# Summing the first two row tiles of an edge table during the load, ahead of the sums in DRAM

## The chip, the cores and the metric

The kernel runs on one core of one Trainium2 chip. The metric is the device time of one execution in microseconds, from the first to the last instruction on the core and what lies around them. The engines have short names in the profile: PE is TensorE (matrix products; PEld is its loading of weights), DVE is VectorE, ACT is ScalarE, POOL is GpSimd, SP is SyncE. DMA transfers are issued by SP, ACT or POOL.

## The reference

One layer of a graph transformer on 1,250 nodes with 768 features, all in float32. Three branches follow each other, cut here to what is computed:

```python
xn = layernorm(x)
x = x + gnn(xn, src, dst) + mix(xn)      # mix: linear attention, then an MLP with gelu
x = x + ffn(layernorm(x))                # 2 of 4 experts, chosen by the mean of all nodes

def gnn(x, src, dst):                    # 21,250 edges, loops of the nodes added to them
    x1 = gat(layer_norm(x), W1, heads=4, width=192)
    x2 = gat(x1, W2, heads=2, width=96)
    return concat(x, x2) @ Wu + bu

def gat(x, W, ...):
    h = x @ W
    e = leaky_relu(s_src[src] + s_dst[dst])
    ee = exp(e - segment_max(e, dst)[dst])
    return segment_sum(ee / segment_sum(ee, dst)[dst] * h[src], dst) + bias
```

What concerns the change is the attention over edges: for each destination node a maximum over its incoming edges, and then a weighted sum. An edge can occur more than once, and counts as often as it occurs.

## The kernel before, in words

**The edges' table.** The kernel turns the list of edges into a dense table of 1,250 by 1,250 counts (row: source node, column: destination node). It is built in DRAM by 170 indirect DMAs of POOL with addition (L315), 125 edges each. They go by turns into two tables, `tabs[0]` and `tabs[1]`, so that a scatter need not wait for the one just ahead of it. `halves[0]` and `halves[1]` are the two tables as 1,250 rows of 1,250 values; `adj_d` is another name for `halves[0]`.

**The two tables become one.** `merged(c)` (L1112) adds the rows of tile c, 125 rows, of the second table to those of the first, with one accumulating DMA from DRAM to DRAM (L1115). Ten such sums make the whole table, 610 KB each.

**The first pass over the table.** `largest` (L1119) finds each destination's maximum, over the ten row tiles. For every tile POOL fetches 610 KB to the chip (`fetch`, L1128), by turns into three buffers: two at the back of `slot_x` and one in `turns`. VectorE makes `far` of it (L1143, no edge becomes a large negative number), and then for each of four heads a running maximum (L1151 for the first tile, L1147 for the others). At the start `before`, here `merged`, is called for tiles 0, 1 and 2, and then `fetch` for tiles 0 and 1. In the loop, step c sums tile c + 3, fetches tile c + 2 and works on tile c. `largest` runs a second time for the second attention layer, with two heads and no sums; it then reads the finished table, as `weighted` does for both layers (L1203).

**What sets the order.** POOL, like each engine, works its instructions in order, and a DMA that has to wait for another one's landing waits on POOL itself. The DMAs of `merged` and `fetch` are held in program order (`pin`). The scatters stand ahead of them on POOL. The work of `gnn` is laid between the steps of the mixing MLP by a credit: `gnn()` is a generator that yields what its last step costs in microseconds, `spend` (L1366) adds to a credit as TensorE's work is written, and takes the next step of `gnn` when the credit is enough. It starts at -44. `largest` yields 9.0 after the first DMAs and 5.0 for every two heads. So VectorE's instructions of `largest` stand at fixed places between those that empty TensorE's banks for the MLP: `fc2_half` (L1077 the products, L1082 the addition of their sum to `slot_a`), and `fc1_unit` (L1046, L1059, L1066).

**The buffers.** `slot_x[:TP, 5000:7500]` holds the first two tiles of three; the running maxima of four heads are in `slot_x[:TP, :5000]`. The queries that lay in `slot_x` before are last read by the projection (L974), which ends before 521 us in the profile.

Of the kernel before, what the change touches and what calls it, by code (L numbers as in the profile page):

```python
# [12 lines left out]
ALU = mybir.AluOpType  # L13
AX = mybir.AxisListType

N, D, TP, NT, KC = 1250, 768, 125, 10, 6
# [16 lines left out]
def tile_gps_layer(ctx, tc, a, out):  # L33
    nc = tc.nc
# [20 lines left out]
    halves = [tab[0:PAIRS, :].rearrange("(s d) o -> s (d o)", d=N) for tab in tabs]  # L55
# [9 lines left out]
    slot_x = big.tile([128, NT * D], F32, name="slot_x")  # L65
# [6 lines left out]
    pin = tc.keep_in_program_order  # L72
# [12 lines left out]
    def bank(name):  # L85
        return p_mm[0].tile([128, 512], F32, name=name, tag="mm")
# [547 lines left out]
    with tc.tile_pool(name="kvp", bufs=1) as kvp:  # L634
# [187 lines left out]
        for t in range(5):  # L822
            def before(t=t):
                if t == 1:
                    by_tokens(vec, xt, TP, TP)
                if t == 2:
                    by_tokens(vec, xt, 2 * TP, 3 * TP)
                    for vv in vvs:
                        pin(nc.vector.memset(vv[:, :, 128:129], 1.0))
# [65 lines left out]
    with tc.tile_pool(name="qp", bufs=1) as qp:  # L895
# [70 lines left out]
        for part in order2:  # L966
# [27 lines left out]
            for t in part:  # L994
                z = qp.tile([TP, D], F32, name="z2", bufs=2)
                i = where[t]
# [111 lines left out]
    def rest(n):  # L1108
        for _ in range(n):
            yield 2.5  # L1110

    def merged(c):  # L1112
        if c < NT:
            cs = slice(c * TP, (c + 1) * TP)
            pin(nc.gpsimd.dma_start(  # L1115
                adj_d[cs, :], halves[1][cs, :], accum_op=ALU.add, max_dma_last_dim=N
            ))

    def largest(heads, s, b_d, pace, before=lambda c: None, behind=lambda: None):  # L1119


        run = slot_x[:TP, : heads * N].rearrange("p (h n) -> p h n", n=N)
        load = [slot_x[:TP, 5000 + i * N : 5000 + (i + 1) * N] for i in range(2)]
        load.append(turns[:TP, 0, :N])

        def fetch(c):
            if c < NT:
                pin(nc.gpsimd.dma_start(load[c % 3], adj_d[c * TP : (c + 1) * TP, :]))  # L1128

        for c in range(3):  # L1130
            before(c)
        fetch(0)
        fetch(1)
        yield 9.0
        for c in range(NT):
            before(c + 3)
            fetch(c + 2)
            if c == NT - 1:
                behind()
            adj = load[c % 3]  # L1140

            far = turns[:TP, 1, :N]
            pin(nc.vector.tensor_scalar(far, adj, -2.0 * NEG, NEG, op0=ALU.mult, op1=ALU.add))  # L1143
            for h in range(heads):
                sc = s[:, 0, h, c : c + 1]
                if c:
                    pin(nc.vector.scalar_tensor_tensor(  # L1147
                        run[:, h, :], far, sc, run[:, h, :], op0=ALU.min, op1=ALU.max
                    ))
                else:  # L1150
                    pin(nc.vector.tensor_scalar(run[:, h, :], far, sc, None, op0=ALU.min))  # L1151
                if h % 2:
                    yield pace
        yield from rest(2)
        mx = gp.tile([TP, heads, NT], F32, name=f"mx{heads}")
        for h in range(heads):
            for u0 in range(0, NT, 4):
                n = min(4, NT - u0)
                ps = bank("ps_mx").rearrange("p (u c) -> p u c", c=128)
                for u in range(n):  # L1160
                    pin(nc.tensor.transpose(
                        ps[:TP, u, :TP], run[:, h, (u0 + u) * TP : (u0 + u + 1) * TP],
                        ident[:TP, :TP],
                    ))
                nc.vector.tensor_reduce(
                    mx[:, h, u0 : u0 + n], ps[:TP, :n, :TP], AX.X, ALU.max
                )
            yield 2.0
        sd = s[:, 1]
        b = gp.tile([TP, 2, heads, NT], F32, name=f"b{heads}")  # L1170
        m = small.tile([TP, heads, NT], F32, name=f"m{heads}", bufs=1)
        nc.vector.tensor_tensor(mx, mx, sd, ALU.add)
        nc.vector.scalar_tensor_tensor(m, mx, 0.2, mx, op0=ALU.mult, op1=ALU.max)
        nc.vector.tensor_tensor(b[:, 0], sd, m, ALU.subtract)
        nc.vector.scalar_tensor_tensor(
            b[:, 1], sd, 0.2, m, op0=ALU.mult, op1=ALU.subtract
        )
        yield from rest(2)
        n = 2 * heads * NT
        ps = bank("ps_row")  # L1180
        pin(nc.tensor.transpose(
            ps[:n, :TP], b.rearrange("p j h t -> p (j h t)"), ident[:TP, :TP]
        ))
        row = small.tile([80, TP], F32, name="row", bufs=1)
        nc.vector.tensor_copy(row[:n], ps[:n, :TP])
        nc.scalar.dma_start(b_d, row[:n])
        yield from rest(4)
# [50 lines left out]
    def gnn():  # L1238
        feats = {}

        def fetch(h):
            gh = turns[:TP, h % 2, :].rearrange("p (t f) -> p t f", f=193)
            pin(nc.gpsimd.dma_start(gh, rows(g1_d[h % 4], TP)))
            feats[h % 4] = gh

        yield from largest(4, s1, b1_d, 5.0, merged, lambda: fetch(0))
        fetch(1)
        for g, (t0, n) in enumerate(SPLITS):
            for h in range(4):
# [15 lines left out]
                for i in range(n):  # L1265
# [9 lines left out]
                    if h == 3:  # L1275
                        for j in range(2):
# [5 lines left out]
                            nc.vector.tensor_reduce(s2[:, j, :, t0 + i], pr, AX.X, ALU.add)  # L1282
        nc.vector.tensor_scalar(s2l, s2[:, 0], 0.2, None, op0=ALU.mult)
        yield from largest(2, s2, b2_d, 4.5)
        load_wu2x()
        parts = earlier()
# [471 lines left out]
    for i in range(6):  # L1758
        for u in range(4):
            q, c = 2 * i + u // 2, u % 2  # L1760
# [100 lines left out]
```

## Time and profile before

| | |
|---|---|
| median of 3 runs | 1902.39 us (1890.05 to 1907.74) |
| the profiled execution | 1900.13 us |
| its span | 1898.2 us |
| TensorE busy | 1869.0 us (98%) |
| VectorE busy | 1336.0 us (70%) |
| POOL busy | 498.0 us (26%), 351.1 of it the 170 scatters of L315 |
| granted TensorE clock | 0.994 of full speed |
| sums in DRAM, L1115 | 10 of 610.4 KB, 12.9 us median to landing |
| fetches of the first pass and the second, L1128 | 20 of 610.4 KB, 6.6 us median to landing |

The page of the profile lists the busy time of each engine, the chain of work that ended last (each step followed back to what released it), the costliest groups of instructions, and the DMA issues. A row of the timeline or the chain begins with the start in microseconds from the span's start, and the duration; in the timeline the engine and the line of the kernel follow, what is written and read, how many such instructions, and in brackets how long the engine stood idle ahead of it and what ended that. A row of the waits reads: who waited, for whom, microseconds in total, times, longest. The releaser named in a wait is inferred; where the engine named had long been done, it was another, often a DMA. The execution profiled has 1.9 us around its span.

### The profile page before, as it was taken

Reading aid. Unit: us, or ns where it says so; the run is one execution under the profiler, and the core shown is the slowest. Engines: PE = TensorE matmul, PEld = TensorE weight load, DVE = VectorE, ACT = ScalarE, POOL = GpSimd, SP = SyncE. Lnnn points to the kernel's source line nnn. Section 1 sums busy time; section 2 is a strip of 40 time slices with the busy share of each in tenths; the row PEclk is TensorE's granted clock in tenths of the full one; section 3 lists DMA queues with packets and bytes.
Section 4 is the critical chain, followed back from the end, with each engine's and each line's share of the span. In section 5 each row is a group of like instructions: output and inputs, shape, how many; then the busy total and the mean of one; then the engine's idle time right before and its main releaser. Section 6 shows DMA issues by size and latency. Waiting matters only on the chain.

```text
span 1898.2 us, 19544 instructions
## 1 busy us (share of the span) xinstructions
PE 1869.0 (98%) x6966; PEld 1245.7 (66%) x6966; DVE 1336.0 (70%) x2407; ACT 803.3 (42%) x1207; POOL 498.0 (26%) x341
## 2 busy tenths in 40 slices
PE   9999999999998999999999999999999999999998
PEld 7555556865565668787777655566766666666664
DVE  4656692677546967676666977766677777777778
ACT  3233221331321128777674186645364353433330
POOL 2265766687882110111111121000221000000000
PEclk9999999999998999999999999999999999999999
DMA  9748532523139751233343532202485201011023
GB/s 341 238 97 213 114 85 52 134 19 49 2 30 187 136 145 55 70 95 88 106 113 79 151 111 73 69 9 67 126 101 82 71 0 67 3 64 47 12 87 109
DMA packets 184285, 175.50 MB, mean 92 GB/s; under 512 B 110043, under 2 KB 153595, under 8 KB 182908
## 3 DMA queue, kind: packets, MB, share of 16 engines
q0 software_dynamic: 126640, 68.01, 20.8%
q1 hardware_dynamic: 54270, 98.48, 16.4%
q10 hardware_dynamic: 3278, 7.75, 1.3%
q8 instruction: 55, 0.90, 0.2%
q14 instruction: 42, 0.34, 0.1%
HBM read 137.80 MB, written 42.05 MB: 95 GB/s over the span
## 4 chain that ended last, share of the span: by engine, by line
PE 91%; DMA 4%; POOL 1%; DVE 1%; issue 1%; ACT 1%; SPq 0%; DVEq 0%; POOLq 0%; ACTq 0%
PE ps_f L1077 14%; PE ps_p L81 13%; PE ps_r L81 12%; PE ps_o L1255 7%; PE ps_a L127 7%; PE ps_g L578 4%; PE ps_u L545 4%; PE ps_p L974 4%; PE ps_c L127 3%; PE ps_f L1655 3%; PE ps_o L1294 2%; PE ps_va L127 2%; PE ps_ka L127 2%; PE ps_qa L127 2%; PE ps_d L127 2%; POOL tab L315 1%
## 5 line engine op out<-in xcount | busy, mean ns | idle before, releaser
L315 POOL DMA_INDIRECT tab<-mult,place_e x170 | 351.1, 2065 | 157.7 <-DMA tab<-mult,place_e 102.6
L1077 PE MATMUL ps_f<-w,v 128*125 128x384 f32 x960 | 338.9, 487 | 6.9 <-DVE slot_a L1082 6.9
L1077 PEld LDWEIGHTS ps_f<-w,v 128*125 128x125 f32 x960 | 178.0, 188 | 113.4 <-DVE slot_a L1082 8.0
L1082 DVE TENSOR_TENSOR slot_a<-ps_f,slot_a 125x384 f32<-125x384 f32 x240 | 131.6, 553 | 66.6 <-PE ps_f L1077 62.7
L1210 DVE TENSOR_TENSOR wt<-ee 125x375 f32<-125x375 f32 (+1 forms) x180 | 105.9, 590 | 84.5 <-PE ps_o L1255 57.5
L1255 PEld LDWEIGHTS ps_o<-turns,wt 125*125 125x125 f32 x800 | 137.1, 188 | 29.1 <-DVE wt L1211 4.0
L1255 PE MATMUL ps_o<-turns,wt 125*125 125x193 f32 x800 | 151.7, 329 | 2.9 <-DVE wt L1211 2.9
L1205 ACT ACTIVATE ee<-bt,s 125x375 f32<-125x375 f32 (+1 forms) x180 | 114.8, 638 | 77.1 <-DVE wt L1210 69.8
L81 PE MATMUL ps_p<-fT,w 128*128 128x312 f32 (+1 forms) x432 | 125.5, 426 | 0.6 <-ACT c L1573 0.6
L1211 DVE SCALAR_TENSOR_TENSOR wt<-wt,slot_x 125x375 f32<-125x375 f32 (+1 forms) x180 | 105.9, 590 | 4.4
L81 PEld LDWEIGHTS ps_p<-fT,w 128*128 128x128 f32 x432 | 81.5, 189 | 36.2 <-ACT c L1573 1.1
L81 PE MATMUL ps_r<-w,slot_a 128*125 128x384 f32 x260 | 94.5, 486 | 0.0
L127 PE MATMUL ps_a<-fT,w 128*128 128x250 f32 (+1 forms) x288 | 86.8, 432 | 0.7 <-DVE slot_a L979 0.7
L1617 DVE SCALAR_TENSOR_TENSOR slot_x<-ps_r,gate,slot_x 125x384 f32<-125x384 f32 x100 | 60.7, 615 | 33.3 <-PE ps_r L81 33.0
L81 PE MATMUL ps_p<-xt,ws 128*128 128x313 f32 (+1 forms) x288 | 83.6, 426 | 0.0
L578 PE MATMUL ps_g<-fx,zT 128*125 128x388 f32 x240 | 80.2, 490 | 1.5 <-DVE zT L372 1.5
L545 PE MATMUL ps_u<-wu,fT 128*125 128x384 f32 x240 | 79.9, 487 | 0.4 <-ACT fT L531 0.4
L974 PE MATMUL ps_p<-wp,slot_x 128*125 128x384 f32 x240 | 79.9, 486 | 0.0
L1147 DVE SCALAR_TENSOR_TENSOR slot_x<-turns,s,slot_x 125x1250 f32<-125x1250 f32 x54 | 79.4, 1512 | 0.1
L1026 ACT ACTIVATE v<-v,par 128x250 f32<-128x250 f32 (+1 forms) x72 | 40.0, 556 | 88.0 <-DVE v L1046 41.3
L1208 ACT ACTIVATE ee<-bt,s1l 125x375 f32<-125x375 f32 (+1 forms) x120 | 75.4, 628 | 0.1
L81 PE MATMUL ps_r<-w2s,ht 128*125 128x384 f32 x200 | 72.7, 486 | 0.0
(403 smaller groups left out, 3413.0 us busy)
## 6 DMA issues: line engine op xcount, KB each, us to landing
turns<-g_d POOLq DMA_DIRECT2D x12, 942.4 KB, 14.2
w<-in_L_mix_fc_w_dram SPq DMA_DIRECT2D x12, 768.0 KB
w<-in_L_mix_fc_w_dram SPq DMA_DIRECT2D x24, 384.0 KB
slot_x<-tab POOLq DMA_DIRECT2D x14, 610.4 KB, 6.6
w<-in_L_ffn_w_dram SPq DMA_DIRECT2D x11, 768.0 KB
w<-in_L_ffn_w_dram SPq DMA_DIRECT2D x5, 1536.0 KB
slot_x<-tab POOLq DMA_DIRECT2D x40, 183.1 KB, 3.3
kr_l<-key_d SPq DMA_DIRECT2D x6, 1062.5 KB
```

What stands on the lines that cost most here:

```text
L81: return lambda *args, **kw: pin(getattr(self.engine, name)(*args, **kw))
L127: engine.matmul(ps, wt[:, k, :], x[:, k, :], start=k == 0 and not more, stop=k == n - 1, skip_group_check=more,)
L315: nc.gpsimd.indirect_dma_start(out=tabs[c % 2][:, :], out_offset=bass.IndirectOffsetOnAxis(ap=place[:, c : c + 1], axis=0), in_=mult[:, c ...
L545: nc.tensor.matmul(ps[:TP, :w], fT[:, k, tc_], wu[:, k, c0 : c0 + w], start=k == 0, stop=k == KC - 1,)
L578: nc.tensor.matmul(ps[:TP, :388], zT[:, k, :], fx[:, k, h2 * 388 : (h2 + 1) * 388], start=k == 0, stop=k == KC - 1,)
L974: nc.tensor.matmul(ps[:TP, :w], qT[:, k, t * TP : (t + 1) * TP], pm[:, k, c0 : c0 + w], start=k == 0, stop=k == KC - 1,)
L1077: nc.tensor.matmul(ps, v_of[c][:, f, h, at : at + TP], lasts[g, j][:, f, :], start=f == 0, stop=f == 1,)
L1082: nc.vector.tensor_tensor(o, ps, o, ALU.add)
L1205: nc.scalar.activation(e[:, 0, :w], bt[:TP, 0, :w], AF.Exp, bias=s[:, 0, h, c : c + 1])
L1210: nc.vector.tensor_tensor(wt[:, :w], e[:, 0, :w], e[:, 1, :w], ALU.max)
L1211: nc.vector.scalar_tensor_tensor(wt[:, :w], wt[:, :w], 1.0, adj, op0=ALU.min, op1=ALU.mult)
L1255: nc.tensor.matmul(sums[i // 2][:TP, (i % 2) * 193 : (i % 2 + 1) * 193], wt[:, i * TP : (i + 1) * TP], gh[:, c, :], start=c == 0 and i % 2 ...
```

## The change

For the first attention layer the first two row tiles do not come from the summed table any more. `merged(0)` and `merged(1)` each load the tile's rows of the first table into the buffer that the fetch filled before, and then load the same rows of the second table on top with an accumulating DMA. `merged(2)` then makes the sums in DRAM of tiles 0, 1 and 2, one after the other, by `merge` (the former `merged`). From tile 3 on `merged(c)` is `merge(c)` as before. `largest` calls `fetch` for tiles 0 and 1 only in its second run, with two heads. All ten sums in DRAM are still made, and all DMAs stay on POOL's queue in program order.

```diff
+    early = [slot_x[:TP, 5000 + i * N : 5000 + (i + 1) * N] for i in range(2)]
+
     def merged(c):
+        if c < 2:
+            rs = slice(c * TP, (c + 1) * TP)
+            pin(nc.gpsimd.dma_start(early[c], halves[0][rs, :]))
+            pin(nc.gpsimd.dma_start(
+                early[c], halves[1][rs, :], accum_op=ALU.add, max_dma_last_dim=N
+            ))
+        for c in ((), (), (0, 1, 2))[c] if c < 3 else (c,):
+            merge(c)
+
+    def merge(c):
         if c < NT:
             cs = slice(c * TP, (c + 1) * TP)
             pin(nc.gpsimd.dma_start(
...
         for c in range(3):
             before(c)
-        fetch(0)
-        fetch(1)
+        if heads == 2:
+            fetch(0)
+            fetch(1)
         yield 9.0
         for c in range(NT):
             before(c + 3)
```

## The prediction

> **What bounds the kernel now.** I read the page first, then the waits, then the chain of waits around the change, then the timeline there. The page's busy table says what a saving must be:
>
> ```profile
> span 1898.2 us, 19544 instructions
> PE 1869.0 (98%) x6966; PEld 1245.7 (66%) x6966; DVE 1336.0 (70%) x2407; ACT 803.3 (42%) x1207; POOL 498.0 (26%) x341
> ```
>
> TensorE is busy 98% of the span, so an edit to transfers is worth what it takes from TensorE's few gaps or adds to them. The waits between 540 and 720 us, where the edges' table is summed and first used, hold the largest gap of the whole run:
>
> ```profile
> DVE turns L1143 <- DMA slot_x<-tab: 10.5, 1, 10.5
> PE ps_f L1077 <- DVE slot_a L1082: 6.9, 1, 6.9
> ```
>
> VectorE stands 10.5 us in front of L1143, the first use of the summed table, until a DMA lands. Behind it in VectorE's order stand the L1082 additions that empty TensorE's banks, so TensorE stops for 6.9 us. The chain of waits shows what the DMA hangs on:
>
> ```profile
> 560.30 3.61 DMA tab<-mult,place_e
> 565.37 17.10 DMA tab<-tab
> 583.19 9.14 DMA slot_x<-tab
> ...
> 595.83 2.92 PE ps_f L1077 x4
> 598.75 3.32 PE ps_a L127 x6
> ```
>
> The last scatter lands at 563.9; the sums of the table in DRAM (tab<-tab, L1115) take to 582.5; the fetch takes to 592.3; TensorE runs again at 595.83. The last two rows also show its clock coming back: four matmuls took 2.92 where eight take 2.58 (1.63 lost), six took 3.32 where six take 1.89 elsewhere (1.43 lost). So this place costs 6.86 + 3.06 = 9.9 us, and no more can be won here. The timeline gives the order of the transfers (POOL issues them in program order) and the use of the first and the third tile:
>
> ```profile
> 564.44 4.63 POOL L1115 DMA_DIRECT2D tab<-tab  x3 [2.14 <-DMA tab<-mult,place_e]
> 576.00 0.57 POOL L1128 DMA_DIRECT2D slot_x<-tab  x1 [6.93 <-PE ps_f L1077]
> 583.19 0.54 POOL L1128 DMA_DIRECT2D slot_x<-tab  x1 [6.63 <-DMA tab<-tab]
> 583.72 1.54 POOL L1115 DMA_DIRECT2D tab<-tab  x1
> 589.42 0.55 POOL L1128 DMA_DIRECT2D turns<-tab  x1 [4.17 <-PE ps_f L1077]
> 590.54 0.96 DVE L1143 TENSOR_SCALAR turns<-slot_x 125x1250 f32<-125x1250 f32 x1 [10.53 <-DMA slot_x<-tab]
> 607.05 0.80 DVE L1143 TENSOR_SCALAR turns<-turns 125x1250 f32<-125x1250 f32 x1
> ```
>
> Three DRAM sums enter the queue at once. By their landings (and the fetches that wait for them) they end at 575.3, 582.5 and 588.8: 10.8 us for the first, then 7.2 and 6.35. The fetch of tile 0 goes out at 576.0 but lies behind sums 1 and 2 and lands only at 590.5. The fetch of tile 2 (the turns row) goes out when sum 2 has landed, with sum 3 ahead of it, and lands at 598.1, 9 us before VectorE wants it at 607.05.
>
> **The change, part by part.** Removed: the fetches of tiles 0 and 1 in the first pass. Added ahead of the three DRAM sums, on POOL: for each of these tiles a plain load of the first table's rows and an accumulating load of the second's. The accumulating load must wait until the plain one has landed, and all that POOL holds behind it waits too: the next pair, and the three DRAM sums, which are all still made because later passes read the summed table. Kept: tile 2 is fetched from DRAM after sum 2, behind sum 3.
>
> *Plain load.* Nearest rows, a fetch of the same 610 KB: 5.0 us on an empty queue (the shortest landing), 6.6 median.
>
> ```profile
> slot_x<-tab POOLq DMA_DIRECT2D x14, 610.4 KB, 6.6
> slot_x<-hx POOLq DMA_DIRECT2D x10, 375.0 KB, 23.0
> tab<-tab POOLq DMA_DIRECT2D x10, 610.4 KB, 12.9
> ```
>
> It needs the first table's scatters alone; the last of those was issued at 558.0 and lands some 3.7 us later, so POOL is free for it at about 562.8. It lands at 562.8 + 5.0 = 567.8.
>
> *Accumulating load.* Not in the trace. From below: a plain load, 5.0. From above: slot_x<-hx, an accumulation into the same memory; its first one took 19.2 us for 375 KB, though with four more behind it and with its source on chip. Nearest: the first DRAM sum, same bytes, same source table, same wait and nothing ahead of it, 10.8 us:
>
> ```profile
> DMA to landing us min/median/max: 10.8/10.8/10.8
> ```
>
> I take 10.84. Below nothing it cannot be: it is one more transfer.
>
> [...]
>
> *The sum.* POOL needs about 0.55 us from a landing to the next issue (575.3 to 576.0 in the trace).
> - Tile 0 is summed at 568.4 + 10.84 = 579.3. VectorE, which stopped at 580.02 before, has it in time: this wait is gone.
> - The load of tile 1 lies behind it in the queue and lands some 1.7 us later (as the fetch of tile 0 landed 1.7 after sum 2): 581.0. Its sum is in at 581.6 + 10.84 = 592.4. VectorE would want it at 596.16 - 9.9 = 586: 6 us late, within the 8.9 us that TensorE ran on after VectorE stopped (580.02 to 588.96). Cost nothing, with that cover; it would be at most 6 us without.
> - The three DRAM sums follow in the same queue at the pace of sums 1 and 2, (7.2 + 6.35) / 2 = 6.8 each: 592.4 + 20.3 = 612.7. Issuing them costs POOL 1.5 us each, beside the transfer of tile 1.
> - Tile 2 lands 9.3 after sum 2, as before (588.8 to 598.1, with sum 3 ahead): 622.0.
> - VectorE wants tile 2 at 607.05 less the lost 9.9 = 597.1 (the additions just ahead of it wait for TensorE, so TensorE's time rules). It waits 24.9 us.
>
> **What is late next is tile 2.** A wait of VectorE costs TensorE 3.65 less (10.53 became 6.86: it runs on for 8.9, and VectorE needs 5.3 to reach the first L1082 again): 21.2, and 3.06 for the clock, 24.3 in all. Less the 9.9 of before: +14.4. Tile 3 is not late: its sum follows at 6.8, VectorE takes some 10 us a tile. Behind the longer wait of POOL stand only transfers of this pass; the scatters are through. Instructions, TensorE's work and bytes stay elsewhere as they are.
>
> Against the profiled execution (span 1898.2, 1.9 around it, 1900.1 in all) this gives 1914.5. The median of the runs shown, 1902.4, lies 2.3 higher: 1916.8, and I forecast 1917. One run is 1890 and one 1908, so about 1% (19 us) is what a measurement of this kernel can tell from no change.
>
> **The rivals.**
> - *Slow sums on chip.* Accumulating into on-chip memory goes as slot_x<-hx did, 19.2 us. Then tile 0 is in at 587.6 (7.5 late as well), and both sums add 2 x 8.4 = 16.7 to tile 2: +31, 1933. For it: the destination is the same memory. Against: that row's source and its four followers.
> - *Short sums, not slower.* One mechanism: the queue drains faster than by sums 1 and 2, which shared it with the fetch of tile 0 and with weights. Sums on chip at 5.0 like a plain load, DRAM sums at 5.1 (the shortest distance of two landings of L1115, 619.8 to 624.9): tile 1 at 580.7, sum 2 at 596.0, tile 2 at 605.3, a wait of 8.2, TensorE loses 4.5 + 3.1, net -2.3: 1900. It decides where tile 2 lands before 607.6; from there on each us is won, down to 1892.5 with no wait. For it: the empty queue. Against: the first DRAM sum had an empty queue too.
> - *No effect:* the wait only changes its place, tile 2 at 607 to 608: the border of the case above, 1902.
>
> **How the numbers follow.** Tile 2 late by about 25 us: 0.54 (1908 to 1925). Slow sums: 0.20 (1925 to 1938). Short sums and no effect: 0.26 (1892 to 1907). Faster by over 1% needs 19 us and only 9.9 are there, so 0.03 for the spread of the runs. Slower by over 1% (above 1921): the slow sums and the upper end of the likeliest case, 0.27. Within: 0.70. The range from 1897 to 1934 leaves out the fullest gain and the slowest sums.
>
> **What would show it.** VectorE's wait at the first L1143 gone or under 3 us; a wait of about 25 us at the third, on the fetch into turns; TensorE's wait on L1082 about 21 us instead of 6.9; accumulating loads of 10 to 12 us; DRAM sums from about 582 on, the last of the three landing near 613. I am wrong if tile 2 comes before 608, or if the first L1143 still waits over 5 us.

## The result and the profile after

The changed kernel takes 1924.66 us (median of four runs, 1920.93 to 1927.56) against 1902.2 us before (four runs, 1890.05 to 1907.74): 1.0124 times as long, 95% interval 1.0096 to 1.0152. The profiled execution took 1923.9 us, its span 1922.1.

The first lines of the page after:

```profile
span 1922.1 us, 19545 instructions
PE 1872.2 (97%) x6966; PEld 1246.2 (65%) x6966; DVE 1338.5 (70%) x2407; ACT 803.0 (42%) x1207; POOL 505.0 (26%) x343
```

The span is 23.9 us longer, and TensorE is busy only 3.2 us longer. So 20.7 us are new gaps in TensorE. The waits between 540 and 740 us hold most of them (L1118 and L1119 are the plain and the accumulating load of a tile, L1128 the sums in DRAM, L1141 the fetches, L1157 the former L1143; the columns are who, for whom, total, times, longest):

```profile
PE ps_f L1077 <- DVE slot_a L1082: 24.8, 4, 11.7
POOL slot_x L1119 <- DMA slot_x<-tab: 20.8, 2, 15.2
DVE turns L1157 <- DMA slot_x<-tab: 16.2, 2, 13.6
DVE turns L1157 <- DMA turns<-tab: 14.9, 1, 14.9
```

TensorE waits 24.8 us for the additions of L1082 instead of 6.9. VectorE waits twice for more than 13 us: for a tile in `slot_x`, and for the third tile, in `turns`. POOL itself stands 15.2 us ahead of an accumulating load. The timelines of POOL and of VectorE say which tile is which:

```profile
561.70 0.63 POOL L1118 DMA_DIRECT2D slot_x<-tab  x1
567.99 3.11 POOL L1119 DMA_DIRECT2D slot_x<-tab  x1 [5.66 <-DMA slot_x<-tab]
569.71 1.98 POOL L1118 DMA_DIRECT2D slot_x<-tab  x1
586.86 3.39 POOL L1119 DMA_DIRECT2D slot_x<-tab  x1 [15.16 <-DMA slot_x<-tab]
588.53 7.79 POOL L1128 DMA_DIRECT2D tab<-tab  x4
621.90 0.56 POOL L1141 DMA_DIRECT2D turns<-tab  x1 [25.57 <-PE ps_f L1077]
```

```profile
583.57 0.81 DVE L1157 TENSOR_SCALAR turns<-slot_x 125x1250 f32<-125x1250 f32 x1 [2.58 <-DMA slot_x<-tab]
589.12 1.00 DVE L1082 TENSOR_TENSOR slot_a<-ps_f,slot_a 125x384 f32<-125x384 f32 x2
603.72 0.81 DVE L1157 TENSOR_SCALAR turns<-slot_x 125x1250 f32<-125x1250 f32 x1 [13.60 <-DMA slot_x<-tab]
627.58 1.14 DVE L1157 TENSOR_SCALAR turns<-turns 125x1250 f32<-125x1250 f32 x1 [14.88 <-DMA turns<-tab]
```

Tile 0 is nearly in time (2.6 us late instead of 10.5). Tile 1 comes at 603.6 and tile 2 at 627.5. The sum of tile 0 went out at 567.99, and the load of tile 1 behind it was in only at 586.6; the row that follows this load on POOL, the sum of tile 1, begins at 586.86, and nothing else was issued meanwhile. The chain of waits runs through these loads, and TensorE restarts twice (two rows of its timeline show the first stop):

```profile
569.71 16.85 DMA slot_x<-tab
586.86 16.77 DMA slot_x<-tab
...
608.04 2.92 PE ps_f L1077 x4
...
621.90 5.58 DMA turns<-tab
```

```profile
594.88 1.45 PE L1077 MATMUL ps_f<-w,v 128*125 128x384 f32 x4
608.04 2.92 PE L1077 MATMUL ps_f<-w,v 128*125 128x384 f32 x4 [11.71 <-DVE slot_a L1082]
```

Each restart is at a low clock again, as the 2.92 for four matmuls shows. The stages' table has the granted clock at 0.69 and 0.74 there (the third number from the right; behind the stretch stand the busy times of TensorE, its weight loads, VectorE, ScalarE and POOL):

```profile
600.00:620.00 20.00, 11.96 (x34) 7.60 (x35) 8.94 (x10) 1.18 (x2) 0.00 (x0) 0.69 1.19 132
620.00:640.00 20.00, 6.88 (x17) 3.18 (x16) 12.39 (x16) 1.37 (x3) 6.82 (x7) 0.74 1.08 175
```

**The 16 landings of a sum.** In these traces a DMA of POOL tells of its landing 16 times. Counted from the issue, in us, by the trace's semaphore events:

| transfer | landings 1 to 11 | landings 12 to 16 |
|---|---|---|
| after: sum of tile 0 on chip, 125 partitions | 6.5 to 8.9 | 15.3, 15.4, 15.5, 15.5, 15.6 |
| after: sum of tile 1 on chip, 125 partitions | 6.8 to 9.2 | 15.7, 15.9, 16.3, 16.3, 16.8 |
| before: first sum in DRAM | 8.2 to 9.7 | 9.8, 10.3, 10.6, 10.8, 10.8 |

Eleven landings of a sum on chip come early and exactly five come over 6 us later. The plain load of tile 1, issued 1.7 us behind the sum of tile 0, has five late landings too (15.4 to 16.9 us after its issue). The sums on chip move in pieces of 1000 bytes, five to a partition, 625 for a tile, and one piece takes 102 ns (median). By these two figures five engines would need 12.75 us for it, 125 pieces each, and sixteen some 4 us (an estimate). The first sum in DRAM of the kernel before shows no such group: its 16 landings lie between 8.2 and 10.8 us. So I formed this theory for the experiments: a sum into 125 partitions is carried by five of the sixteen DMA engines. The view of the DMA queues from 578 to 580 us, in the midst of the sum of tile 0, fits it (packets, MB, and the time of the packets as a share of 16 engines'):

```profile
q0 software_dynamic: 125, 0.12, 39.3%
```

### The profile page after: what moved, and what is told of

The parts are those of the page before. It is cut to its first block, busy times and chain, and to the rows that moved or that the text cites. A ratio compares the mean times of both kernels' runs of the same rounds, so it can differ in the third digit from the quotient of the medians.

```text
span 1922.1 us, 19545 instructions
## 1 busy us (share of the span) xinstructions
PE 1872.2 (97%) x6966; PEld 1246.2 (65%) x6966; DVE 1338.5 (70%) x2407; ACT 803.0 (42%) x1207; POOL 505.0 (26%) x343
## 3 DMA queue, kind: packets, MB, share of 16 engines
q0 software_dynamic: 130672, 69.29, 21.2%
## 4 chain that ended last, share of the span: by engine, by line
PE 91%; DMA 4%; DVE 2%; ACT 1%; issue 1%; ACTq 0%; POOL 0%; DVEq 0%; POOLq 0%
PE ps_f L1077 14%; PE ps_p L81 13%; PE ps_r L81 12%; PE ps_a L127 7%; PE ps_o L1269 7%; PE ps_u L545 4%; PE ps_p L974 4%; PE ps_c L127 3%; PE ps_g L578 3%; PE ps_f L1669 3%; PE ps_o L1308 2%; DMA slot_x<-tab 2%; PE ps_va L127 2%; PE ps_ka L127 2%; PE ps_qa L127 2%; PE ps_d L127 2%
## 5 line engine op out<-in xcount | busy, mean ns | idle before, releaser
L1077 PE MATMUL ps_f<-w,v 128*125 128x384 f32 x960 | 342.4, 491 | 24.9 <-DVE slot_a L1082 24.8
L1082 DVE TENSOR_TENSOR slot_a<-ps_f,slot_a 125x384 f32<-125x384 f32 x240 | 131.6, 553 | 67.6 <-PE ps_f L1077 63.9
L1269 PEld LDWEIGHTS ps_o<-turns,wt 125*125 125x125 f32 x800 | 137.1, 188 | 30.4 <-DVE wt L1225 5.2
L1269 PE MATMUL ps_o<-turns,wt 125*125 125x193 f32 x800 | 151.7, 329 | 4.2 <-DVE wt L1225 4.2
## 6 DMA issues: line engine op xcount, KB each, us to landing
slot_x<-tab POOLq DMA_DIRECT2D x16, 610.4 KB
```

The source lines that it names most:

```text
L1077: nc.tensor.matmul(ps, v_of[c][:, f, h, at : at + TP], lasts[g, j][:, f, :], start=f == 0, stop=f == 1,)
L1082: nc.vector.tensor_tensor(o, ps, o, ALU.add)
L1269: nc.tensor.matmul(sums[i // 2][:TP, (i % 2) * 193 : (i % 2 + 1) * 193], wt[:, i * TP : (i + 1) * TP], gh[:, c, :], start=c == 0 and i % 2 ...
```

## The experiments

Two theories on why the sums on chip take 16 us stood against each other: five engines do the work; or adding into chip memory, or POOL's queue with its round trips, is slow as such. A second question was how much of the loss is the place of the sums in DRAM. Each ratio is to the kernel before on the chip of the experiment, where its median was 1898.26 us (71 runs) or, for the 100 partitions, both mends, the addition by VectorE and the kernel before once more, 1905.61 (14 runs); it stands with its 95% interval, and need not be the quotient of two medians.

**Sixteen engines for the sum.**

```diff
-            pin(nc.gpsimd.dma_start(
-                early[c], halves[1][rs, :], accum_op=ALU.add, max_dma_last_dim=N
-            ))
+            for p0, p1 in ((0, 112), (112, TP)):
+                pin(nc.gpsimd.dma_start(
+                    early[c][p0:p1], halves[1][c * TP + p0 : c * TP + p1, :],
+                    accum_op=ALU.add, max_dma_last_dim=N
+                ))
```

> The changed kernel, but each accumulating load is two DMAs, partitions 0 to 111 and 112 to 124. Theory (five engines): with 125 partitions the sum into chip memory runs on 5 of the 16 DMA engines, 125 pieces of 1000 bytes each at 102 ns = 12.8 us, and five of its 16 landings come 7 us after the others; with 112 and 13 partitions it runs on 16 and 13 engines, so that a sum lands 9 to 10 us after its issue instead of 15.6 and 16.8, the third tile comes at about 615 us instead of 627.5, and the time is 1906 to 1912. Rival (adding into chip memory is slow by itself, or POOL's descriptors are): landings stay at 15 to 17 us or grow with the second DMA, time 1922 to 1928.

Measured: 1906.52 us, ratio to before 1.0044 (1.0028 to 1.0061); the change itself has 1.0124. The sums now land fast, sooner than the 9 to 10 us expected. The view of their line:

```profile
L1120 POOL DMA_DIRECT2D slot_x<-tab x4: 1392/1485/1540, 564.5 to 576.0; - x4
...
DMA to landing us min/median/max: 6.2/6.5/8.0
```

The 16 landings of the 112 partitions come together, between 5.6 and 6.7 us after the issue; the bytes, the pieces of 1000 bytes, the destination and the addition are those of the changed kernel. Both parts of a tile are in 7.1 and 8.9 us after the first one's issue. So neither adding on chip nor POOL's issue is slow as such. In 2 us in the midst of the sum of tile 0 (568 to 570) the queue now moves three times as many pieces:

```profile
q0 software_dynamic: 378, 0.38, 121.9%
```

The share of over 100% says that the records of packets overlap somewhat; if 121.9 stands for sixteen engines, the 39.3 of the changed kernel stands for 5.2. So this estimate, without the landings, comes to five engines too. The stop at tile 1 is gone; the one for tile 2 (in at 610.9, with the last scatter 2.8 us earlier than in the changed kernel's profile) is left:

```profile
616.42 2.92 PE L1077 MATMUL ps_f<-w,v 128*125 128x384 f32 x4 [8.57 <-DVE slot_a L1082]
```

**What sets the number of engines.** The same with `((0, 100), (100, TP))`.

> The changed kernel with accumulating loads of 100 and 25 partitions, to see what sets the number of engines. Theory (the largest divisor of the partitions up to 16): 100 partitions run on 10 engines, 50 pieces of 1000 bytes each, 5.1 us; with the 3 us around it a landing of 8 to 8.7 us, ten of 16 landings late; 25 partitions run on 5 engines, 25 pieces, 2.6 us. Rival (only the multiple of 16 matters, or one DMA of 125 is slow for another reason): 100 partitions land in 6.7 us like 112, or in over 12.

Measured: one execution, 1910.91 us. Tile 2 came at 617.7, and TensorE stopped 16.5 us at L1082. The sums of 100 partitions landed after 10.0 and 10.4 us, between those of 112 and of 125:

| partitions of a sum | early landings | late landings |
|---|---|---|
| 112 (first tile) | none | 16, at 5.6 to 6.7 us |
| 100 (first tile) | 5 at 4.1 to 5.0, 1 at 6.5 | 10 at 8.0 to 10.0 us |
| 125 (first tile of the change) | 11 at 6.5 to 8.9 | 5 at 15.3 to 15.6 us |

Ten late landings for 100 partitions, five for 125, all for 112: these three counts fit the largest divisor of the partitions up to sixteen. That is my reading of three counts; for DMAs of 13 and of 25 partitions no count stands here. (The number of pieces, 500, 625 and 560, has the same divisors, so these runs don't tell the two apart.) The expected 8 to 8.7 us were too few: eight of the ten late landings came in that time, the last one at 10.0. The 25 partitions behind them may have shared engines with them; the two were not tried apart.

**The sum without its addition.**

```diff
-            pin(nc.gpsimd.dma_start(
-                early[c], halves[1][rs, :], accum_op=ALU.add, max_dma_last_dim=N
-            ))
+            pin(nc.gpsimd.dma_start(early[c], halves[1][rs, :]))
```

> The changed kernel, but the second load of tiles 0 and 1 is a plain load into the same buffer (the first table's counts are left out of these two tiles in the first pass); the waits and the order of the queue stay. Theory: the accumulation is the cost, so the second load lands in 5 to 6 us, tile 1 is in at about 582, the third tile at about 609, time 1901 to 1906. Rival (the round trips through POOL's queue and the two extra transfers are the cost, whatever they do): the third tile still comes after 618 and the time stays above 1914.

Measured: 1903.50 us, ratio 1.0012 (0.9991 to 1.0034). The second loads:

```profile
DMA to landing us min/median/max: 5.3/5.5/5.7
```

Tile 1 was in at 581.5 and tile 2 at 610.4. The interval holds 1 and ends at 1.0034, so the round trips through POOL's queue alone make at most a small part of the loss; but tile 2 is still late, and TensorE stops 9.1 us for it in one piece (6.9 at tile 0 in the kernel before). The plain load of tile 0 in the changed kernel, also into 125 partitions, has its 16 landings from 4.3 to 5.4 us after its issue. So with no sum ahead of it this plain load has no late landings, and the accumulating load that follows it has five. The edit takes away the addition and `max_dma_last_dim` together, and the pieces become 5000 bytes; which of these makes the second load fast was not tried apart. A sum in two parts on chip took 7.1 and 8.9 us in all where this plain load took 5.7 and 5.3.

**The sum of tile 2 ahead of those that nobody needs yet.**

```diff
-        for c in ((), (), (0, 1, 2))[c] if c < 3 else (c,):
+        for c in {0: (), 1: (), 2: (2,), NT + 2: (0, 1)}.get(c, (c,)):
             merge(c)
```

> The changed kernel, but the sum in DRAM of tile 2 comes first, and those of tiles 0 and 1 come behind all the others. Theory: the second stop of TensorE (11.3 us and the clock) comes from the two sums in DRAM that lie ahead of tile 2 and that nobody needs yet; tile 2 comes at about 618 instead of 627.5, VectorE waits under 5 us for it, the first stop of 11.7 us stays, time 1911 to 1915. Rival (tile 2 is late because the whole queue is slow after the accumulating loads): time above 1919.

Measured: 1906.14 us, ratio 1.0042 (1.0026 to 1.0058), better than expected. The waits of this kernel, 560 to 700 us:

```profile
DVE turns L1157 <- DMA slot_x<-tab: 14.6, 2, 12.8
PE ps_f L1077 <- DVE slot_a L1082: 10.6, 2, 10.0
DVE turns L1157 <- DMA turns<-tab: 0.9, 1, 0.9
```

Tile 2 lands at 611.9 and VectorE waits 0.9 us for it. I had expected 618, from the pace of sums that share the queue; with one sum ahead of it the fetch took 5.3 us. The stop for tile 1 (10.0) is left, with its cause, the sums on chip of 15.5 and 16.0 us. So each of the two stops has its own cause, and each mend takes one of them away; in time each brings the ratio from 1.0124 down to about 1.004.

**Both mends.**

> The changed kernel with both mends: accumulating loads of 112 and 13 partitions, and the DRAM sum of tile 2 ahead, those of tiles 0 and 1 behind all the others. Theory: tiles 0 and 1 at about 572 and 584, tile 2 at about 598 to 600, no stop of TensorE or one under 1 us, time 1890 to 1896, as with the fetch sooner. Rival (the on-chip sums cost the queue what the order saves): tile 2 after 603 and 1898 or more.

Measured: 1903.27 us beside 1905.61 for before on that chip, ratio 0.9997 (0.9971 to 1.0024). The profiled execution, with 1896.56 us one of the shortest of ten, has tiles 0 and 1 at 579.5 and 589.4 and tile 2 at 604.0; VectorE waits 2.0 and 5.5 us, TensorE 5.2 us in three pieces. Its last scatter went out at 563.8, 4.3 us later than in the changed kernel's profile. My figures were too early, and the rival holds as far as this goes: with both mends the change can't be told from no change.

**The kernel before with another order.** The first of two attempts at something better than both kernels:

```diff
-        for c in range(3):
-            before(c)
+        before(0)
+        before(1)
         fetch(0)
+        before(2)
         fetch(1)
```

> The kernel before with one change of order on POOL: sum 0, sum 1, fetch 0, sum 2, fetch 1, in place of sums 0, 1, 2, fetch 0, fetch 1. Theory: the wait of 10.5 us of before was fetch 0 lying behind sum 2 in the queue; it lands at about 584 instead of 590.5, VectorE waits 4 to 5 us, TensorE under 2 us, time 1893 to 1897. Rival (the wait is the time of the sums themselves): no change, 1900 to 1904.

Measured: 1893.36 us beside 1898.26 for before, ratio 0.9982 (0.9967 to 0.9996). TensorE doesn't stop at L1082 between 575 and 660 us in this profile, and tile 0 is used at 582.01 without a wait. But the last scatter of that execution went out at 553.0, 7.3 us earlier than in the profile of before, which helps too. That the order alone saves is shown by the ratio, if narrowly (the interval ends at 0.9996): 3.4 us of 1898 by it, less than the 9.9 of the one profile of before.

**The first tile added by VectorE.** The second attempt, from the kernel before: two plain loads and an addition on chip for tile 0, the sums in DRAM from tile 1 on, that of tile 0 last.

```diff
     def merged(c):
+        if c == 0:
+            pin(nc.gpsimd.dma_start(slot_x[:TP, 5000 : 5000 + N], halves[0][:TP, :]))
+            pin(nc.gpsimd.dma_start(turns[:TP, 0, :N], halves[1][:TP, :]))
+        else:
+            merge(0 if c == NT + 2 else c)
+
+    def merge(c):
         if c < NT:
...
-        fetch(0)
+        if heads == 2:
+            fetch(0)
         fetch(1)
         yield 9.0
         for c in range(NT):
+            adj = load[c % 3]
+            if c == 0 and heads == 4:
+                pin(nc.vector.tensor_tensor(adj, adj, load[2], ALU.add))
             before(c + 3)
             fetch(c + 2)
             if c == NT - 1:
                 behind()
-            adj = load[c % 3]
```

> The kernel before, but tile 0 is loaded plainly from both tables, into its buffer and into the third tile's buffer, and VectorE adds the two (1.5 us more of its work); the sums in DRAM go 1, 2, 3 and so on, that of tile 0 last. Theory: no accumulation stands ahead of the first tile, both loads land by 570 us, tile 1 by 586, tile 2 by 593, no stop of TensorE near L1082, time as with the fetch sooner, 1890 to 1896. Rival (the third tile's fetch waits for VectorE's addition and comes late): a wait of VectorE at the third tile, time 1898 or more.

Measured: 1891.47 us (five runs) beside 1905.61, ratio 0.9929 (0.9903 to 0.9954). It beats both kernels. The edit also takes the sum in DRAM of tile 0 out of the front of the queue; what of the gain is that, and what the sum by VectorE, was not tried apart. Its waits from 560 to 700 us:

```profile
DVE turns L1153 <- DMA slot_x<-tab: 4.9, 1, 4.9
PE ps_f L1077 <- DVE slot_a L1082: 2.2, 2, 1.2
```

This was the longest of the five executions (1896.61 us), with the last scatter at 566.7, the latest of all ten profiles: tile 0 was still in time (both loads in at 578.2), tile 1 came 4.9 us late and TensorE lost 2.2. The loads landed 8 us later than I had expected, since the scatters did. The third tile's fetch did not wait for VectorE.

**The kernel before once more.**

> The kernel before, unchanged, once more with a profile. Its runs spread from 1889 to 1911 us. Theory: the wait for the first tile differs from run to run with the order in which scatters, sums and fetches share the queue, so that this profile's own time and its wait at L1143 move together, about one us of time for one of TensorE's stop. Rival: the spread comes from elsewhere, and the stop is again 6 to 8 us whatever the time.

Measured: 1897.95 us. The waits there:

```profile
DVE turns L1143 <- DMA slot_x<-tab: 6.6, 1, 6.6
PE ps_f L1077 <- DVE slot_a L1082: 2.8, 1, 2.8
```

TensorE stopped 2.8 us instead of 6.9, and the execution was 2.2 us shorter than the first profiled one. Tile 0 landed at the same time (590.6); TensorE and VectorE arrived some 4 us later, so the wait was shorter. That is half of what was expected: the stop differs from run to run, but not one for one with the time, and not because of the queue's order. What makes the spread of 20 us is open.

## Why the prediction was right, and where it was off

**Right: the wait moves, it doesn't go.** The wait at the first tile fell from 10.5 to 2.6 us (forecast: under 3), the third tile became late behind three sums in DRAM that stand in a queue held up by the accumulating loads, and the kernel became slower. The range from 1897 to 1934 holds the time; the likeliest value of 1917 is 7.7 us too low, and slower by over 1% had the lesser chance.

**Near the mark partly by luck.** TensorE's stops came to 24.8 us where 21.2 were forecast, but they lie elsewhere: the forecast had nothing at tile 1 and all of it at tile 2, measured are 11.7 at tile 1 and 13.1 at tile 2. What tile 1 cost more, tile 2 in part cost less. Of the signs that I had named, the wait at the first tile and TensorE's total came; the wait for the third tile was 14.9 instead of about 25, the accumulating loads took 15.6 and 16.8 instead of 10 to 12, and the last of the three sums in DRAM landed at 621.3 instead of near 613.

**The term that was mis-sized: the accumulating load.** I took 10.84 us from the first sum in DRAM; measured are 15.56 and 16.77. The choice of the nearest row failed: the sum in DRAM moves in 1,250 pieces and all its landings lie within 2.6 us, the sum on chip has five of its 16 landings over 6 us behind the other eleven. Why the sum in DRAM, also of 125 rows, has no such group is open. The row that I used as the upper bound, slot_x<-hx, has the same destination and the same 125 partitions, and the trace of before holds its 16 landings: eleven 5.4 to 6.3 us after the issue, five from 10.5 to 19.2. Its 19.2 was not all followers, as I had argued.

**Step by step.**

| step | forecast | measured |
|---|---|---|
| plain load of tile 0 in | 567.8 | 567.1 |
| tile 0 summed | 579.3 | 583.6 |
| load of tile 1 in | 581.0 | 586.6 |
| tile 1 summed | 592.4 | 603.6 |
| third DRAM sum in | 612.7 | 621.3 |
| tile 2 in | 622.0 | 627.5 |
| TensorE's stops at L1082 | 21.2, once | 24.8, in two large pieces of 11.7 and 11.3 |

**The second term: tile 1 was put at nothing.** The two slow sums put tile 1 at 603.6, 11 us later than forecast. But the step was wrong in itself too. I set a wait of 6 us against a cover of 8.9 us of TensorE's own work and called it free; by the rule that I used for tile 2 (a wait of VectorE costs TensorE 3.65 us less, as the 10.53 of before became 6.86), 6 us would have cost some 2.4. And the cover was smaller than at tile 0: VectorE stopped at 590.1 and TensorE at 596.3, 6.2 us later, and from the tile's arrival to TensorE's restart it took another 4.3. So the wait of 13.6 cost TensorE 11.7, only 1.9 less. VectorE came to tile 2 only at 612.7, so its wait there was 14.9 instead of 24.9. Two steps went the other way: the three DRAM sums took 17.7 us instead of 20.3, and the fetch of tile 2 landed 6.2 after the third instead of 9.3, because sum 3 had been in the queue so long that it was nearly through (13 of its 16 landings were in when the fetch went out). One row of the chain of before was misread without effect on the sum: the fetch that lands at 592.3 is that of tile 1; VectorE waited for tile 0's, in at 590.5.

**The sum.** Forecast were 14.4 us more, the span shows 23.9. The starts of the same matmuls in the two timelines tell where. Ahead of the change TensorE is already 1.0 us later than before (580.23 and 579.26), behind the stops 20.5 (642.72 and 622.27), at the first products of `weighted` 22.0 (736.25 and 714.25), at the end 23.9. So the place of the change holds 19.5 us: 17.9 of longer stops, and some 1.6 for the clock, which came back twice and not once. The forecast was 3.6 short in the stops (24.8 against 21.2) and had no second restart. Whether the 3.4 us behind the place (1.3 of it a longer wait at L1269, 4.2 instead of 2.9) follow from the change is open.

**The rivals.** Of the two cases for the cost of a sum the slow one was nearer, though with 16 us and not 19.2. Short sums did not happen; that a fast queue would have been enough only to come even is shown by the plain second load, with 1.0012 and tile 2 at 610.4 (the same sum with 5.0 us for the load, and the DRAM sums at the pace I forecast, would give 610.3).

## What to carry to other kernels

When a producer is replaced by a nearer one, follow the first consumer that still depends on the old path: here tile 2, behind sums that nobody needed yet. Price an accumulating DMA by a row with the same destination and the same number of partitions, and look at all its landings, not the last alone; 125 partitions in two DMAs of 112 and 13 were in after 7 to 9 us where one took 16. Where VectorE has the time, two plain loads and one addition (1.45 us) can be the cheaper sum; here they were part of the kernel with the lowest ratio.

## What the runs showed of the hardware

- An accumulating load of 610 KB into 125 partitions lands after 15.5 to 16.8 us, with five late landings of 16; two of them into 112 and 13 partitions are both in 6.9 to 8.9 us after the first issue (four tiles in two profiles); a plain load of the same bytes with no sum ahead of it lands after 5.3 to 5.7 us (the 16 landings of the changed kernel's first one lie from 4.3 to 5.4 us).
- Pieces of 1000 bytes of a sum on chip took 102 ns each (median), pieces of 500 bytes of a sum in DRAM 65 ns.
- The end of the scatters differs by 14 us between profiles with the same scatters: the last went out at 553.0 us at the earliest and 566.7 at the latest. Why is open.
